# A decoder kernel of twelve layers: the last feed-forward in bf16 terms, the ternary feed-forward by groups, and shared statistics in the last cross attention

## The chip, the cores and the metric

The kernel runs on one core of one Trainium2 chip. The engines of a core work side by side and are ordered by semaphores: PE (TensorE, matrix products and transposes), DVE (VectorE), ACT (ScalarE), POOL (GpSimd) and SP (SyncE, which issues DMAs here). The metric is the device time of one execution in microseconds, as the median of several runs.

## The reference

`x` has 2 x 1024 tokens of 256 features. Twelve layers follow each other, four blocks of attention, cross attention and feed-forward, each as `x = layernorm(x + layer(x))` with eps 1e-5 and no gain. Three of them, and the norms between them, are touched by the change.

The feed-forward of the second block quantises its activations to 8 bits per token and its weights to three values:

```python
def bitlinear(x, w, b):
    xn = rmsnorm(x)                    # x * rsqrt(mean(x*x) + 1e-6)
    xq = activation_quant(xn)          # round(xn * 127/max|xn|), clipped, divided again
    wq = weight_quant(w)               # -1, 0, 1 times mean|w|
    return einsum('bsi,oi->bso', xq, wq) + b
h = gelu(bitlinear(x, w1, b1)); out = bitlinear(h, w2, b2)      # 256 -> 1024 -> 256
```

The cross attention of the last block normalises `x` (which has just been normalised by the block's layernorm) a second time, with a gain and a bias, makes queries from it, and keys and values both from it and from a context of 154 masked rows of 192 features. Queries and keys are normalised per head (4 heads of 64); the output is projected and `bo` is added.

The feed-forward of the last block has weights quantised to -1, 0 and 1 without a scale, and activations in full precision:

```python
def _quantize(W):
    gamma = mean(abs(W))
    return clip(round(W / (gamma + 1e-5)), -1.0, 1.0)
h = relu(einsum('bsd,fd->bsf', x, _quantize(W1)) + b1)          # 256 -> 1024
out = einsum('bsf,df->bsd', h, _quantize(W2)) + b2              # 1024 -> 256
```

## The kernel before

`x` stays in SBUF through all layers as 16 tiles (NT) of 128 tokens by 256 features in float32. A layer's method does the layer; `run` calls them in turn and loads the next layer's weights while one works (`after_loads`, which returns the next layer's weights). After each residual addition `stats` makes a tile's mean and variance (`mv`). Where a layer isn't `by_tile` or `grouped`, `run` then calls `post_norm`: one square root on ACT for all 16 tiles, one reciprocal on DVE, and sixteen DVE operations `(x - mean) * r` in place, 128x256 each. A layer named in `LAZY` is left without it, and the next layer does the norm itself. `centred` is the same operation for one tile with a given `r`, and `twin_roots` makes both roots that two norms in a row need from one set of variances, by integer and Newton steps on DVE alone; both were there for the first feed-forward.

A scheduler orders the instructions of each engine from the program's order, their dependencies and a cost model. `in_order(since)` binds PE to the program's order; this is done in several stages, the last cross attention among them, and not in the two feed-forwards here. PSUM is given out as banks by name: four `pa`, two `pt`, two `po` in the feed-forwards.

`l1_ffn` works on four groups of four tiles. `first(g)` takes the absolute maxima of the group (L1352), scales to 8-bit integers in float32 (`xq`, L1357), rounds (L1359) and casts to bf16 (`xi`, L1348), and POOL adds the output's bias `b2` to `x` (L1358). `second` transposes a tile on PE, multiplies by the bf16 ternary weights, scales and biases `h` on DVE (L1376), and does the GELU and the sums of squares on ACT. `third`, one group later, quantises `h`, transposes and multiplies again and adds to `x` (L1395). `first(g + 1)` is called after all four tiles of group `g`.

`l3_xattn` prepares the context (`l3_context`, `l3_turned_context`), the pairs of tiles (`l3_pair`: statistics, root on POOL by a power, `xn` on DVE at L2202, `bo` added to `x` on POOL at L2204, transposes, ACT with gain and bias at L2211, then keys and values in `l3_keys`) and queries (`l3_queries`). These are generators that `flights` takes a step at a time. The root of the context, `crs`, is also POOL's (L2117, L2119). Then come 8 units of ten blocks of keys: scores on PE, exponentials on ACT (L2329), products with the values (L1898), DVE sums (`acc`, L1903) and the next unit's maxima on PE and DVE (L2290). The rest of the preparation, `later`, is taken in steps between the blocks.

`l3_ffn` transposes `x` to `xT` (`start_features`, 16 tiles), quantises both weights in place in float32 (`ternary`: absolute sum L1293, then three operations L1298 to L1300 over 128x2048), and for each of four groups of 512 tokens does eight products of 128x512 (two float32 matmuls each) with ReLU on ACT (L1946), then four tiles of eight float32 products and one for the bias row (`row_pair`), added to `x` at L321. After it `run` normalises all tiles (L329) and issues sixteen output DMAs on SP (L2844).

## Time and profile before

| what | us |
|---|---|
| runs: median (lowest to highest of 3) | 3605.53 (3596.46 to 3615.26) |
| the profiled execution, its own time | 3597.27 |
| its span | 3595.5 |
| mean granted PE clock | 0.908 |
| busy: PE / DVE / ACT / POOL | 3086.0 / 1739.3 / 1274.3 / 398.1 |
| start of l1_ffn: reciprocal of the norm / first `xi` | 1915.33 / 1932.88 |
| last cross attention: first norm operation / first context root used | 3008.30 / 3023.22 |
| last feed-forward: first / last matmul product | 3455.58 / 3582.98 |
| first output DMA issued | 3585.23 |

Rows of a group read: line, engine, operation, output <- inputs, shapes, count, then busy time and mean ns of one, then idle time of the engine just before them with what ended it. Rows of a timeline read: start, duration, engine, line, operation, names, shapes, count, and in brackets the idle time before with its releaser. PEld is the weight load of PE. A busy PE is not PE at its peak, since ends of matmuls are modelled.

### The profile page before, as it was taken

The page shows a single profiled execution, that of the slowest core. Times are in us where ns is not written, and L with a number is a line of the kernel's source. Part 1 is how long each engine was busy: PE and PEld are TensorE (multiplying, and loading weights), DVE is VectorE, ACT ScalarE, POOL GpSimd, SP SyncE. Part 2 cuts the span into 40 slices and gives each one's busy share as a digit, 9 for nine tenths or more (in the row PEclk, how much of TensorE's full clock was granted, in tenths as well). Part 3 has the DMA queues.
Part 4 walks back from the last instruction along what each step waited for, and adds up shares of the span by engine and source line. Part 5 has one row for each costly group of instructions (what it writes and reads, how often), then busy time and mean ns, then how long its engine had stood idle before and what let it go on. Part 6 is the DMA issues. An engine that isn't in the chain of part 4 may idle for free.

```text
span 3595.5 us, 57974 instructions
## 1 busy us (share of the span) xinstructions
PE 3086.0 (86%) x24289; PEld 1896.1 (53%) x24296; DVE 1739.3 (48%) x3889; ACT 1274.3 (35%) x2319; POOL 398.1 (11%) x510
## 2 busy tenths in 40 slices
PE   8997889989959997688895699999798786899978
PEld 3554556654459997576432456454475343443345
DVE  2366775434541112797668665100201765567741
ACT  3553345434411111597344523111022443333321
POOL 0000000010012332100001131000021202110000
PEclk9998779789969999799997799999799897999989
DMA  3234523100058886000000001100133000000000
GB/s 96 80 83 124 130 73 88 34 1 1 24 205 322 316 326 220 1 2 33 1 1 8 8 1 72 59 0 0 57 129 127 19 1 27 1 1 1 1 0 24
DMA packets 152542, 242.19 MB, mean 67 GB/s; under 512 B 47059, under 2 KB 127450, under 8 KB 147290
## 3 DMA queue, kind: packets, MB, share of 16 engines
q1 hardware_dynamic: 140874, 115.67, 10.9%
q0 software_dynamic: 11408, 122.83, 8.9%
q8 instruction: 191, 3.13, 0.4%
q14 instruction: 69, 0.57, 0.1%
HBM read 195.07 MB, written 43.38 MB: 66 GB/s over the span
## 4 chain that ended last, share of the span: by engine, by line
PE 71%; DVE 17%; ACT 5%; issue 3%; POOL 2%; DMA 2%; SPq 0%; POOLq 0%; DVEq 0%; ACTq 0%
PE pa L253 29%; PE po L253 9%; PE po L1898 2%; PE wide L741 2%; PE wide L2324 2%; PE pa L1573 2%; PE po L823 1%; PE wide L2289 1%; PE wide L253 1%; PE pt L295 1%; PE px L253 1%; PE po L2584 1%; PE y_ps L2637 1%; PE pa L1459 1%; PE wide L711 1%
## 5 line engine op out<-in xcount | busy, mean ns | idle before, releaser
L253 PEld LDWEIGHTS pa<-xgT,ew 128*128 128x128 f32 x2184 | 251.7, 193 | 2.8 <-DVE xgT L967 0.8
L253 PE MATMUL pa<-xgT,ew 128*128 128x128 f32 x2184 | 252.0, 276 | 0.4 <-DVE xgT L967 0.4
L253 PE MATMUL pa<-xT,w 128*128 128x512 f32 (+3 forms) x488 | 236.6, 627 | 4.0 <-DVE x L321 1.8
L253 PE MATMUL pa<-ha,w 128*128 128x512 f32 x512 | 220.4, 592 | 0.0
L985 DVE TENSOR_TENSOR hid<-a,pa 128x512 f32<-128x512 f32 x78 | 48.4, 621 | 294.6 <-ACT a L984 294.6
L253 PEld LDWEIGHTS pa<-ha,w 128*128 128x128 f32 x512 | 97.3, 190 | 122.5 <-issue 122.5
L746 ACT ACTIVATE e<-wide 77x1024 f32<-77x1024 f32 x128 | 124.2, 1016 | 104.4 <-PE wide L741 101.3
L2744 DVE COPY lg<-po 128x8 f32<-128x8 f32 x16 | 2.7, 167 | 302.1 <-PE po L2741 302.1
L253 PE MATMUL po<-w,h 128*128 128x256 f32 (+1 forms) x640 | 144.5, 382 | 0.0
L253 PEld LDWEIGHTS pa<-xT,w 128*128 128x128 f32 (+2 forms) x488 | 87.1, 190 | 105.9 <-issue 97.0
L253 PEld LDWEIGHTS po<-w,h 128*128 128x128 f32 (+1 forms) x640 | 113.2, 179 | 30.6 <-issue 8.5
L984 ACT ACTIVATE a<-pa 128x512 f32<-128x512 f32 x78 | 42.4, 544 | 234.1 <-PE pa L253 234.1
L253 PE MATMUL po<-ew,hid 128*128 128x256 f32 x546 | 125.3, 379 | 0.0
L295 PE MATMUL pt<-cst,x 128*128 128x128 f32 x224 | 52.1, 339 | 82.4 <-DVE x L2079 53.8
L715 DVE TENSOR_REDUCE m<-wide 128x4 f32<-128x616 f32 x128 | 95.6, 792 | 44.8 <-PE wide L711 44.6
L2329 ACT ACTIVATE e<-wide 128x1024 f32<-128x1024 f32 x64 | 65.5, 1023 | 116.9 <-PE wide L2324 116.2
L253 PEld LDWEIGHTS po<-ew,hid 128*128 128x128 f32 x546 | 100.2, 190 | 11.8
L2290 DVE TENSOR_REDUCE m<-wide 128x2 f32<-128x1024 f32 (+1 forms) x96 | 90.7, 968 | 18.3 <-PE wide L2289 18.3
L1147 ACT ACTIVATE e<-cst,wS,nS 128x80 f32<-128x80 f32 x256 | 95.3, 449 | 0.0
L2289 PE MATMUL wide<-kT,qT 64*128 64x512 f32 (+1 forms) x384 | 86.5, 532 | 6.6 <-DVE m L2290 5.7
L1580 ACT ACTIVATE hb<-pa,cols 128x512 f32<-128x512 f32 x32 | 22.0, 687 | 197.8 <-PE pa L253 197.8
L1903 DVE TENSOR_TENSOR acc<-acc,e 128x1024 f32<-128x1024 f32 (+1 forms) x64 | 78.1, 1221 | 27.4 <-ACT e L2329 19.7
(649 smaller groups left out, 6430.4 us busy)
## 6 DMA issues: line engine op xcount, KB each, us to landing
w<-in_L2f_eW_dram SPq DMA_DIRECT2D x16, 1024.0 KB, 6.4
pk<-pk SPq DMA_DIRECT2D x96, 128.0 KB, 2.2
rw<-pk SPq DMA_DIRECT2D x64, 128.0 KB, 2.7
y<-yd SPq DMA_DIRECT2D x16, 512.0 KB, 5.5
ld<-lgs SPq DMA_DIRECT2D x64, 64.0 KB, 2.2
li<-ld SPq DMA_DIRECT2D x16, 256.0 KB, 4.7
md<-mi SPq DMA_DIRECT2D x32, 128.0 KB, 3.8
mt<-md SPq DMA_DIRECT2D x64, 64.0 KB, 1.8
```

What stands on the lines that cost most here:

```text
L253: self.nc.tensor.matmul(out, l, r, start=(i == 0), stop=(i == n - 1))
L295: self.nc.tensor.transpose(ps[:, c * 128:(c + 1) * 128], src[:, c * 128:(c + 1) * 128], self.ident)
L715: nc.vector.tensor_reduce(m[:, t, 2 * k:2 * k + 2, G0:G0 + 2], s, AX.X, ALU.max)
L741: nc.tensor.matmul(pair[j // 2][:KH, j % 2 * 512:j % 2 * 512 + 512], kp[R, G, o:o + KH], tiles[g][R, G], start=True, stop=True)
L746: nc.scalar.activation(s, pair[k][:KH], AF.Exp, scale=0.25)
L1147: nc.scalar.activation(e[:, 4 * j + G], self.k("rel"), AF.Tanh, scale=nS[:, i, h:h + 1], bias=wS[:, i, h:h + 1])
L1573: nc.tensor.matmul(ps, w["rW1"][:, c, m * 128:(m + 1) * 128], self.xT[:, c, cols], start=(c == 0), stop=(c == 1))
L1898: nc.tensor.matmul(av[a * 64:a * 64 + 64], v[:rows, n, h:h + 64], e[:rows, a * 512:a * 512 + 512], start=(s == 0), stop=(s == 9))
L1903: nc.vector.tensor_tensor(acc[:rows], acc[:rows], e[:rows], ALU.add)
L2289: nc.tensor.matmul(wide[:, a * 512:a * 512 + size], qT[R, c, o:o + 128], kT[R, c, keys], start=(n < 2), stop=True)
L2290: nc.vector.tensor_reduce(m[:, t, :, n], wide.rearrange("p (a k) -> p a k", a=2)[:, :, :size], AX.X, ALU.max)
L2324: nc.tensor.matmul(wide[:rows, a * 512:a * 512 + 512], kT[R, c, o:o + rows], qT[R, c, q], start=False, stop=True)
```

## The change

Five things change, in this order of the diff.

`l1_ffn`: the layer before it, `l1_xattn`, becomes lazy; the root is made at the start of `l1_ffn`, and the tiles are centred group by group in `first(g)`. The bias is added by one DVE operation per group, `biased(g)`, called after the group's first tile, in place of four POOL operations; `first(g + 1)` is called after the group's second tile.

`l3_xattn`: `l3_attn` becomes lazy; `twin_roots` makes the roots of the block's norm and of the layer's own norm. `l3_pair` makes `xn` from the raw `x` with the one root, and normalises `x` in place with the other; POOL still adds `bo`.

`l3_weights`: the quantisation of the last feed-forward's weights is handed to the attention's `later`, in steps over halves of 128x1024, and ends in bf16 in the place of the float32 weights.

`l3_ffn`: the features and the hidden values are split into three bf16 terms each (`terms`: a difference, a cast, a difference on DVE, where ACT has written the highest term), and each product is six (up) or 24 (down) bf16 matmuls. The bias `b2` is added to `x` by POOL, 128x256 each. The down products of a group come after the up products of the next group and the transposes of the one after, and PE is bound to this order.

The end: `l3_ffn` is lazy, and each tile gets its root, its norm and its output DMA in the loop, one tile behind.

```diff
@@ -1338,7 +1338,9 @@
             ms = p1.tile([128, NT], F, name="ms")
             top = p1.tile([128, NT], F, name="top")
 
-            nc.vector.tensor_tensor(ms, self.norm, self.norm, ALU.mult)
+            norm = p1.tile([128, NT], F, name="norm")
+            self.rstd(norm, self.mv[:, :, 1], self.eps5)
+            nc.vector.tensor_tensor(ms, norm, norm, ALU.mult)
             nc.vector.tensor_tensor(ms, ms, self.mv[:, :, 1], ALU.mult)
             nc.vector.tensor_scalar(ms, ms, 1e-6, None, ALU.add)
             ms = self.newton_root(p1, ms, NT)
@@ -1349,17 +1351,22 @@
 
             def first(g):
                 tiles = slice(g * 4, g * 4 + 4)
+                for i in range(g * 4, g * 4 + 4):
+                    self.centred(self.x[:, i], i, norm[:, i:i + 1])
                 nc.vector.tensor_reduce(top[:, tiles], self.x[:, tiles], AX.X, ALU.max, apply_absolute_value=True)
                 sc = self.l1_scales(p, ms[:, tiles], top[:, tiles], g1)
                 xq = p.tile([128, 4, D], F, name="xq")
                 for k in range(4):
                     i = g * 4 + k
                     nc.vector.tensor_scalar(xq[:, k], self.x[:, i], ms[:, i:i + 1], sc[:, k:k + 1], ALU.mult, ALU.mult)
-                    nc.gpsimd.tensor_tensor(self.x[:, i], self.x[:, i], w["b2"], ALU.add)
                 nc.vector.tensor_scalar(flat(xq), flat(xq), -128.0, ROUND, ALU.max, ALU.add)
                 xi = p.tile([128, 4, D], BF, name="xi")
                 ints(flat(xi), flat(xq))
                 return xi
+
+            def biased(g):
+                tiles = slice(g * 4, g * 4 + 4)
+                nc.vector.tensor_tensor(self.x[:, tiles], self.x[:, tiles], w["b2"].unsqueeze(1).to_broadcast([128, 4, D]), ALU.add)
 
             def second(g, k, xi, hm, ht):
                 i = g * 4 + k
@@ -1395,7 +1402,7 @@
                 nc.vector.scalar_tensor_tensor(self.x[:, i], ps[:, :D], ht[:, k:k + 1], self.x[:, i], ALU.mult, ALU.add)
                 self.finish(i)
 
-            behind = None
+            behind = ahead = None
             xi = first(0)
             for g in range(5):
                 if g < 4:
@@ -1407,8 +1414,11 @@
                         hs.append(second(g, k, xi, hm, ht))
                     if behind:
                         third(g - 1, k, *behind[k])
-                if g < 3:
-                    xi = first(g + 1)
+                    if k == 0 and g < 4:
+                        biased(g)
+                    if k == 1 and g < 3:
+                        ahead = first(g + 1)
+                xi = ahead
                 if g < 4:
                     nc.vector.tensor_scalar(hm, hm, 1e-6, None, ALU.add)
                     hm = self.newton_root(p, hm, 4)
@@ -1834,7 +1844,7 @@
 
 
         nc, tc = self.nc, self.tc
-        after_loads()
+        following = after_loads()
         self.psum_close()
         cp = self.psum_cx = ExitStack()
         PS = bass.MemoryType.PSUM
@@ -1845,6 +1855,7 @@
         with ExitStack() as cx:
             p1 = cx.enter_context(tc.tile_pool(name="x1", bufs=1))
             p = cx.enter_context(tc.tile_pool(name="x2", bufs=2))
+            self.twin = self.twin_roots(p1, 1e-5)
             k = self.l3_context(p1)
             qT = p1.tile([128, 2, T], F, name="qT")
             batches = [(p.tile([128, 2, SK + S], F, name="kT"), p.tile([128, 10, D], F, name="v")) for _ in range(B)]
@@ -1873,6 +1884,8 @@
             self.bank = self.pa
             later = self.flights([query(4), query(6)] + pairs(1) + [self.l3_keys(p, 1, 0, batches[1], w, k)]
                                      + [query(i) for i in range(8, NT, 2)], 3)
+            weights = self.l3_weights(p1, following)
+            later = (x for g in (later, (x for _ in weights for x in (True, True))) for x in g)
             order = list(range(2, 10)) + [0, 1]
             score = lambda u, s, sh: self.l3_scores(p, units[u], order[s], qT, batches[units[u][0]], k, sh)
             behind, oT = [], None
@@ -1928,26 +1941,74 @@
         w = {m: self.load(s, self.ins[f"L3f_{m}"]) for m in ("W1", "W2")}
         w["raw1"] = s[0][:, 0:2048]
         w["raw2"] = s[0][:, 2048:4096]
-        w["b2"] = self.rows(s, "L3_ffn_b2", D)
+        w["b2"] = self.rows_all(s, "L3_ffn_b2", D)
+        w["spare"] = s[0][:, 4096 + D:4608 + D]
         return w
 
     def l3_ffn(self, w, after_loads):
+
+
         nc, tc = self.nc, self.tc
         after_loads()
-        self.start_features()
+        rs = self.rs
+        since = len(nc.cur_bb.bb.instructions)
         with tc.tile_pool(name="t1", bufs=2) as p:
-            self.ternary(p, w["raw1"], w["raw1"], 1024 * D, True)
-            self.ternary(p, w["raw2"], w["raw2"], 1024 * D, True)
-            for g in range(4):
-                h = p.tile([128, 8, 512], F, name="h")
+            self.rstd(rs, self.mv[:, :, 1], self.eps5)
+
+            def features(g):
+                xt = [p.tile([128, 2, 512], BF, name=f"xt{j}") for j in range(3)]
+                for i in range(g * 4, g * 4 + 4):
+                    nc.vector.tensor_scalar(self.x[:, i], self.x[:, i], self.mv[:, i, 0:1], rs[:, i:i + 1], ALU.subtract, ALU.mult)
+                for k in range(4):
+                    i = g * 4 + k
+                    tile_of = slice(k * 128, k * 128 + 128)
+                    pt = self.transpose_pair(self.x[:, i])
+                    v = self.xT[:, :, i * 128:(i + 1) * 128]
+                    nc.scalar.copy(v, pt)
+                    nc.scalar.copy(xt[0][:, :, tile_of], pt)
+                    self.terms([t[:, :, tile_of] for t in xt], v, high=False)
+                for i in range(g * 4, g * 4 + 4):
+                    nc.gpsimd.tensor_tensor(self.x[:, i], self.x[:, i], w["b2"], ALU.add)
+                return xt
+
+            def up(g, xt):
+                h = [p.tile([128, 8, 512], BF, name=f"h{j}") for j in range(3)]
                 for m in range(8):
                     ps = self.pa()
-                    self.mm(ps, [(w["W1"][:, c, m * 128:(m + 1) * 128], self.xT[:, c, g * 512:(g + 1) * 512]) for c in range(2)])
-                    nc.scalar.activation(h[:, m], ps, AF.Relu, bias=self.col("L3_ffn_b1", m))
+                    self.mm(ps, [(w["q1"][:, c, m * 128:(m + 1) * 128], t[:, c]) for c in range(2) for t in xt])
+                    f = p.tile([128, 512], F, name="f", bufs=3)
+                    nc.scalar.activation(f, ps, AF.Relu, bias=self.col("L3_ffn_b1", m))
+                    nc.scalar.activation(h[0][:, m], ps, AF.Relu, bias=self.col("L3_ffn_b1", m))
+                    self.terms([t[:, m] for t in h], f, high=False)
+                return h
+
+            def ended(i):
+                nc.vector.tensor_scalar(self.x[:, i], self.x[:, i], self.mv[:, i, 0:1], rs[:, i:i + 1], ALU.subtract, ALU.mult)
+                nc.sync.dma_start(self.out[i * 128:(i + 1) * 128], self.x[:, i])
+
+            def down(g, h):
                 for k in range(4):
+                    i = g * 4 + k
                     ps = self.po()
-                    self.mm(ps[:, :D], [(h[:, m, k * 128:(k + 1) * 128], w["W2"][:, m]) for m in range(8)] + [self.row_pair(w["b2"])])
-                    self.residual(g * 4 + k, ps[:, :D])
+                    self.mm(ps[:, :D], [(t[:, m, k * 128:(k + 1) * 128], w["q2"][:, m]) for m in range(8) for t in h])
+                    nc.vector.tensor_tensor(self.x[:, i], self.x[:, i], ps[:, :D], ALU.add)
+                    self.stats(i)
+                    nc.scalar.activation(rs[:, i:i + 1], self.mv[:, i, 1:2], AF.Sqrt, bias=self.eps5)
+                    if i:
+                        ended(i - 1)
+                    nc.vector.reciprocal(rs[:, i:i + 1], rs[:, i:i + 1])
+                ended(i) if i == NT - 1 else None
+
+            xt = features(0)
+            behind = up(0, xt)
+            xt = features(1)
+            for g in range(1, 5):
+                h = up(g, xt) if g < 4 else None
+                if g < 3:
+                    xt = features(g + 1)
+                down(g - 1, behind)
+                behind = h
+            self.in_order(since)
 
     NB = 2 * NT + NE - 1
 
@@ -2192,15 +2253,13 @@
 
         nc = self.nc
         i = b * TPB + 2 * j
-        r = self.rs[:, i:i + 2]
-        for t in range(2):
-            self.stats(i + t)
-        self.inverse_root(r, self.mv[:, i:i + 2, 1], self.eps5.to_broadcast([128, 2]), 2)
-        yield True
+        r = self.twin
         xn = p.tile([128, 2, D], F, name="xn", bufs=3)
         for t in range(2):
-            nc.vector.tensor_scalar(xn[:, t], self.x[:, i + t], self.mv[:, i + t, 0:1], self.rs[:, i + t:i + t + 1],
-                                    ALU.subtract, ALU.mult)
+            self.centred(xn[:, t], i + t, r[:, 1, i + t:i + t + 1])
+        yield True
+        for t in range(2):
+            self.centred(self.x[:, i + t], i + t, r[:, 0, i + t:i + t + 1])
             nc.gpsimd.tensor_tensor(self.x[:, i + t], self.x[:, i + t], w["bo"], ALU.add)
         yield True
         ps = self.bank()
@@ -2814,12 +2873,52 @@
     def centred(self, dst, i, r):
         self.nc.vector.tensor_scalar(dst, self.x[:, i], self.mv[:, i, 0:1], r, ALU.subtract, ALU.mult)
 
+    def l3_weights(self, pool, w):
+
+        nc = self.nc
+        w["q1"] = w["raw1"][:, 0:1024].bitcast(BF).rearrange("p (c n) -> p c n", n=1024)
+        w["q2"] = w["raw2"][:, 0:1024].bitcast(BF).rearrange("p (c n) -> p c n", n=D)
+        keep = w["spare"].bitcast(BF)
+        for n in (1, 2):
+            raw, q = w[f"raw{n}"], w[f"q{n}"]
+            r = pool.tile([128, 4], F, name=f"tern{n}")
+            for k in range(2):
+                nc.vector.tensor_reduce(r[:, k:k + 1], raw[:, k * 1024:k * 1024 + 1024], AX.X, ALU.add, apply_absolute_value=True)
+                yield True
+            nc.vector.tensor_tensor(r[:, 2:3], r[:, 0:1], r[:, 1:2], ALU.add)
+            yield True
+            ps = self.pa()
+            self.mm(ps[:, 0:1], [(self.k("ones"), r[:, 2:3])])
+            nc.vector.tensor_scalar(r[:, 3:4], ps[:, 0:1], 1.0 / (D * 1024), 1e-5, ALU.mult, ALU.add)
+            nc.vector.reciprocal(r[:, 3:4], r[:, 3:4])
+            yield True
+            flat = q.rearrange("p c n -> p (c n)")
+            for k in range(2):
+                half = raw[:, k * 1024:k * 1024 + 1024]
+                nc.vector.tensor_scalar(half, half, r[:, 3:4], 1.0, ALU.mult, ALU.min)
+                yield True
+                nc.vector.tensor_scalar(half, half, -1.0, ROUND, ALU.max, ALU.add)
+                yield True
+                nc.vector.tensor_scalar(flat[:, 1024:2048] if k else keep, half, -ROUND, None, ALU.add)
+                yield True
+            nc.vector.tensor_copy(flat[:, 0:1024], keep)
+            yield True
+
+    def terms(self, dst, src, high=True):
+
+        nc = self.nc
+        if high:
+            nc.vector.tensor_copy(dst[0], src)
+        nc.vector.tensor_tensor(src, src, dst[0], ALU.subtract)
+        nc.vector.tensor_copy(dst[1], src)
+        nc.vector.tensor_tensor(dst[2], src, dst[1], ALU.subtract)
+
 
     LAYERS = ("l0_attn", "l0_xattn", "l0_ffn", "l1_attn", "l1_xattn", "l1_ffn",
               "l2_attn", "l2_xattn", "l2_ffn", "l3_attn", "l3_xattn", "l3_ffn")
 
 
-    LAZY = ("l0_xattn",)
+    LAZY = ("l0_xattn", "l1_xattn", "l3_attn", "l3_xattn", "l3_ffn")
 
     def run(self):
         loads = [getattr(self, "load_" + n) for n in self.LAYERS]
@@ -2840,8 +2939,6 @@
             if not self.fed and name not in self.LAZY:
                 self.post_norm()
             w = nxt[0] if nxt else None
-        for i in range(NT):
-            self.nc.sync.dma_start(self.out[i * 128:(i + 1) * 128], self.x[:, i])
         self.psum_close()
```

## The prediction

> **What bounds the kernel now.** I read the page's head and the chain of waits first, then tables by stage for the four places that the change touches, then groups and timelines there.
>
> ```profile
> PE 3086.0 (86%) x24289; PEld 1896.1 (53%) x24296; DVE 1739.3 (48%) x3889; ACT 1274.3 (35%) x2319; POOL 398.1 (11%) x510
> PE 71%; DVE 17%; ACT 5%; issue 3%; POOL 2%; DMA 2%; SPq 0%; POOLq 0%; DVEq 0%; ACTq 0%
> ```
>
> PE carries the chain as a whole, but these shares say little of single stages. In the table by stage the columns are the stretch, its length, the busy time of PE, PEld, DVE, ACT and POOL, and the granted clock:
>
> ```profile
> 1910.00:1934.00 24.00, 3.51 (x19) 2.81 (x18) 22.07 (x69) 1.05 (x2) 3.93 (x5) 0.64 0.10 28
> 3326.00:3361.00 35.00, 32.41 (x168) 11.10 (x168) 26.58 (x29) 12.42 (x14) 0.00 (x0) 1.00 0.01 1
> 3440.00:3456.00 16.00, 4.96 (x17) 3.47 (x18) 14.99 (x31) 1.42 (x4) 0.00 (x0) 0.50 0.00 1
> 3456.00:3583.00 127.00, 126.99 (x436) 78.45 (x434) 20.22 (x54) 23.62 (x37) 0.00 (x0) 0.99 0.00 0
> 3583.00:3596.00 13.00, 0.00 (x0) 0.00 (x0) 6.54 (x20) 0.31 (x1) 0.00 (x0) 0.60 0.48 161
> ```
>
> Start of l1_ffn (row 1): DVE bound. One unit of the last cross attention (row 2): PE bound, DVE 8 us free. Last feed-forward: 16 us DVE bound at half clock, 127 us pure PE, and a tail of 13 us without PE. The groups of the last stage, and its end:
>
> ```profile
> L253 PE MATMUL po<-w,h 128*128 128x256 f32 x256 | 59.1, 384 | 0.0
> L253 PE MATMUL pa<-xT,w 128*128 128x512 f32 x128 | 58.6, 609 | 0.0
> L1946 ACT ACTIVATE h<-pa,cols 128x512 f32<-128x512 f32 x32 | 22.0, 687 | 83.8 <-PE pa L253 83.8
> L1293 DVE TENSOR_REDUCE tr<-w 128x1 f32<-128x2048 f32 x2 | 4.6, 2276 | 0.0
> ...
> 3583.02 0.42 DVE L321 TENSOR_TENSOR x<-x,po 128x256 f32<-128x256 f32 x1 [3.18 <-PE po L253]
> 3584.79 5.25 DVE L329 TENSOR_SCALAR x<-x,mv,rs 128x256 f32<-128x256 f32 x16
> 3585.23 7.74 SPq L2844 DMA_DIRECT2D out_dram<-x  x16
> ```
>
> Rows that price the new operations: bf16 matmuls at half clock (8 in 3.60 us) and at full clock (8 in 1.05 us), and DVE beside a working POOL and alone.
>
> ```profile
> 1942.75 3.60 PE L253 MATMUL pa<-w,xqT 128*128 128x512 bf16 x8 [4.82 <-ACT xqT L1370]
> 1965.99 1.05 PE L253 MATMUL po<-w,hT 128*128 128x256 bf16 x8 [0.99 <-ACT hT L1392]
> 1928.56 2.19 DVE L1357 TENSOR_SCALAR xq<-x,root,qsc 128x256 f32<-128x256 f32 x4
> 1929.05 2.96 POOL L1358 TENSOR_TENSOR x<-x,w 128x256 f32<-128x256 f32 x4 [130.58 <-DVE xq L1357]
> 1932.88 0.68 DVE L1348 TENSOR_SCALAR xi<-xq 128x1024 bf16<-128x1024 f32 x1
> L1903 DVE TENSOR_TENSOR acc<-acc,e 128x1024 f32<-128x1024 f32 x6 | 7.3, 1222 | 1.9 <-ACT e L2329 1.9
> ```
>
> A DVE scaling of 128x256 costs 0.33 us in a run (5.25/16) and 0.55 beside POOL (2.19/4).
>
> **A. l1_ffn.** Before, recip at 1915.33, 16 scalings (5.25), four reductions of 1.21 and the Newton steps put the first xq at 1928.56; POOL's four bias adds (0.72 each) then stretch xq by 0.22 x 4 and the next small operations to 0.68, so xi comes at 1932.88. After, twelve scalings and three reductions fit ahead of xq (−0.33 x 4 −1.2 = −2.5; some small operations fall into gaps, −0.9), and without POOL xq, 1359 and xi shrink by about 2; the new bias addition of 128x1024 (1.22) stands between. First xi −4. The remaining group's work comes later, where PE waits for DVE, and takes 1 back. Groups 2 and 3 lose the contention of POOL (two rows of 3.44 us) for one addition of 1.22: −1.5 each. Sum −6; bounds −9 (nothing is taken back) and −3 (only the lead-in's scalings count).
>
> **B. Last cross attention's lead-in.** Before: last aggregate 3007.6, then sqrt, recip, 16 scalings to 3013.5, statistics anew, POOL power 0.72 per pair; POOL's crs ends 3023.18 and holds the context (DVE idle 3.85 us). After: 13 small dependent DVE operations at 0.21 (2.7), then 20 scalings, half in place, for ten tiles; each in-place one frees a POOL add of bo (0.72). Ten of these stand in POOL's queue before the mask casts (2.4) and crs (1.2): from 3011 to 3018–3021, crs at 3022–3024.7, against 3023.2. So DVE's earlier end is not passed on; late next is crs. Four ternary reductions (1.21) lie here in the idle of DVE. Behind it POOL has no eps and power per pair (0.19+0.72) ahead of the query roots, worth 0 to 4. Two table loads and one sqrt less are off the path. I take −2; bounds −6, +3.
>
> **C. Ternary weights moved into the attention loop.** Removed from the last stage: two reductions 2.28, six scalings of 128x2048 (1.2–1.27) on DVE, of which 4.6+3.7 stood before the first transposes. Added: in each of two units a burst of six scalings 128x1024 (0.60) and a bf16 copy, 4.2 us. A unit is 34.7 us with DVE 26.6–27.1 busy; its chain alternates PE, DVE maximum, ACT, so a burst delays some maximum: +2 each, +4. Bounds 0 (it fits into 8 us idle) and +9 (fully exposed). The scale's matmul with the ones waits for DVE's sum, and the scores of the next unit are queued behind it on PE; the sum is 0.2 us and a step earlier, so I cost it at nothing, and at 1.2 (one DVE addition in front) without that cover.
>
> **D. Last feed-forward, up and down.** Lead-in: before, last residual ends 3439.2, first up matmul 3455.6 (16.4). After: statistics 0.61, sqrt 0.31, recip 0.25, six scalings 2.0, then per tile transposes, two ACT copies 0.37, DVE difference, cast, difference of 128x256 (0.9) with two scalings between: 8 us to the first up. Gain 8.4; bounds 4 (tile pitch 1.15 at half clock, as the copies at 3450.28 and 3451.43 had) and 9.5.
>
> PE: a group's up is 48 bf16 matmuls of 128x512; half of the half-clock 0.43 is 0.215, 10.3 us (before 13.8). A down tile is 24 of 0.12 (1.05/8 = 0.13 with one start in it), 2.9, four 11.5, against 4.27 x 4 = 17.1. DVE per m: difference 0.61 (half of 1.22), cast 0.34 (half of 0.68), difference 0.61 = 1.56, more than PE's 1.29 or ACT's two relus at 0.69. First group to second up: nothing else covers, so DVE sets it: 2.7 + 8 x 1.56 + four tiles at 0.9 = 18.8. Middle steps: up 10.3, transposes waiting for ACT 3.9, down 11.5 = 25.7, twice; DVE has 12.5+4+6.4 = 23 there and stays just below. Last: 10.3+11.5+11.5 = 33.4. Sum 103.6. PE waits some 6 us after the first up; such a wait (idle to 3449.5) left it at half clock until 3458, so +2. POOL now adds b2 (16 x 0.72), and beside it DVE runs 1.7 times as long: +2. Total 107.6 against 127.4 (3455.6 to 3583.0): −19.8; bounds −27 (no wait, full clock) and −8 (per m 1.9, steps 28).
>
> [...]
>
> **E. Tail.** Before 12.5 us from last PE end 3583.0 to 3595.5: residual to aggregate 1.1, sqrt and recip 0.6, then sixteen DMA issues 7.74 and 2.5. After, fourteen tiles are gone by then; the last: 1.1 + 0.6, two scalings 0.7 (the tile before goes first), one issue 0.5, 2.5 = 5.4. Gain 7.1; bounds 5 (an earlier transfer is still queued) and 8. Inside the stage each tile's recip now waits for ACT's sqrt (0.31), with DVE's next differences queued behind it; the scaling of the tile before covers it, and without that cover it is 16 x 0.35, inside R1's margin. SP has nothing else queued.
>
> **Sum.** −6 −2 +4 −8.4 −19.8 −7.1 = −39.3, on the profiled execution's 3597.27: 3558.0. That execution lies 8.3 below the median 3605.53, near the lowest of the three shown (3596.46 to 3615.26); against the median the sum gives 3566. I take 3562, midway, and put the rivals on the same base, 3601. A measurement of this kernel tells about 0.5% (18 us) from no change.
>
> **Rivals.** R1, DVE becomes the bound of the last stage: with 2.3 us per m (1.5 times, near the contended ratio) DVE needs 32 x 2.3, 16 x 1 for features, 16 x 1.6 for residual, statistics and scaling, and 2.7: 118; D's middle gains 9, the bursts cost 9: −6 −2 +9 −8.4 −9 −7.1 = −24, 3577. For: DVE's margin is only 2.7 us a step. Against: POOL works 2.9 us a group only.
> R2, three times the matmuls eat what bf16 saves: bf16's 0.215 x 6 = 1.29 per m against 1.72 leaves little, and if DVE's and ACT's waits leave steps near 31 only lead-in, tail and A's lower bound count, with C at +9: −9.5, within 0.5%, 3592. Against: the 1.05 us row.
> R3, slower: the last stage runs like l1_ffn, whose bf16 matmuls with waits between had 8 in 3.60 us. At 0.45 and 0.236 a step is 21.6+22.7+4 = 48; four give 193, +66, less lead-in, tail and A to C: +46, 3647. It decides once the stage's mean granted clock is below 0.61: 97 us of PE work / 0.61 + 6.6 = 165, which is 127.4 + 15.5 + 4 + 18. Against: PE has 24 us of work in 26.
>
> **How the numbers follow.** Likeliest 0.60, its own range 3545 to 3579 (the bounds of A to E added in squares, about 13, and half the distance of the two bases, 4). R1 0.20, R2 0.11, R3 0.09. Range 3538 to 3594: it takes R1 and most of R2, leaves R3 and a tenth below out. Faster by over 0.5% is below 3587.5: the first, most of R1, little of R2: 0.80; within 0.5% 0.12; slower 0.08.
>
> **What would show it.** Right: first up about 8 us after the last residual; second up 19 later; steps of 25 to 27 with PE busy over 90% and a clock near 1; last PE to end 5 us; first h of l1_ffn 4 to 6 earlier; units with a burst 36 to 37 long. Wrong: DVE busy without a break over the last stage, a clock below 0.7 there, or units 5 us longer, or crs later than the sum of the lead-in.

## The result, and the profile after

The changed kernel takes 3568.64 us (median of 5 runs, 3564.39 to 3574.31) against 3605.53 us (5 runs, 3596.46 to 3615.26). The ratio is 0.991 with a 95% interval of 0.988 to 0.994. The prediction was 3562 us in a range of 3538 to 3594.

The profiled execution has a span of 3565.6 us (before 3595.5) and a mean granted clock of 0.904 (before 0.908). The first row of its page:

```profile
PE 3062.2 (86%) x24445; PEld 1882.0 (53%) x24456; DVE 1802.5 (51%) x4036; ACT 1301.2 (36%) x2387; POOL 413.1 (12%) x494
```

PE has 24 us less to do and DVE 63 us more. Where the time went is read from the starts and ends of the instructions that bound each stage, in the timelines of both profiled executions. "Unit" is one of the eight units of the last cross attention, and a unit ends where ACT's copy of its products (`avs`) begins.

| stretch | before | after | difference | predicted |
|---|---|---|---|---|
| start to the last statistic of l1_xattn (no change in it) | 1914.95 | 1920.81 | +5.86 | |
| A: from there to the first query copy of the next layer | 153.17 | 149.28 | -3.89 | -6 (-9 to -3) |
| from there to the last residual of l3_attn (no change in it) | 938.63 | 938.03 | -0.60 | |
| B: from there to the end of unit 0 | 135.80 | 130.29 | -5.51 | -2 (-6 to +3) |
| unit 1 | 61.45 | 61.45 | 0 | 0 |
| C: units 2 to 7 | 219.77 | 232.41 | +12.64 | +4 (0 to +9) |
| from there to the last residual of l3_xattn | 15.45 | 15.45 | 0 | 0 |
| D: from there to the last PE instruction | 143.77 | 112.78 | -30.99 | -28.2 |
| E: from there to the end | 12.51 | 5.06 | -7.45 | -7.1 |

The five changed stretches sum to -35.2 us; the prediction had -39.3. Over all the profiled executions of this study the first stretch lies between 1893 and 1926 us, with the same code in it. The changed stretches repeat within 0.1 us where their code is the same, but for two: B, which has two levels (130.2 to 130.9 and 132.5 to 132.8 us), and D, which lies between 112.0 and 113.1. In five of the seven kernels with the higher level of B the unchanged stretch ahead of it is about 2 us shorter (935.4 to 935.8 against 937.7 to 938.1), so there B and that stretch together come out the same. So the experiments below are read by stretch and not by a whole time.

The tables by stage of the changed kernel, for the places that the prediction showed (columns as there; the stretches are l1_ffn's start, units 3 and 5, and the lead-in, body and tail of the last feed-forward):

```profile
1916.00:1938.00 22.00, 4.47 (x21) 3.14 (x21) 19.08 (x68) 3.04 (x5) 0.00 (x0) 0.65 0.12 31
3250.48:3290.38 39.90, 34.77 (x168) 11.80 (x168) 30.42 (x38) 12.18 (x14) 0.00 (x0) 0.92 0.00 0
3333.14:3369.52 36.38, 33.80 (x166) 11.45 (x166) 26.57 (x29) 12.17 (x14) 0.00 (x0) 0.95 0.01 1
3447.72:3457.85 10.13, 4.12 (x11) 1.76 (x13) 9.65 (x27) 2.71 (x9) 3.05 (x4) 0.50 0.00 1
3457.85:3560.50 102.65, 90.90 (x593) 59.51 (x595) 87.33 (x213) 51.22 (x103) 31.78 (x12) 0.95 0.06 19
3560.50:3565.60 5.10, 0.01 (x1) 0.00 (x0) 1.61 (x5) 0.29 (x1) 0.00 (x0) 0.87 0.15 51
```

Row 3 is a unit in which nothing of the change runs (DVE as busy as before, 26.57), and still it is 1.64 us longer than before, at a clock of 0.95 instead of 1.00. Row 5 is the last feed-forward's body: PE busy for 89%, DVE for 85%, the clock 0.95. The groups of that stage, and from the timeline of DVE its end:

```profile
L253 PE MATMUL pa<-xt,w 128*128 128x512 bf16 x188 | 47.1, 407 | 8.7 <-DVE xt L2913 6.3 <-POOL x L1971 0.8 <-ACT xt L1968 0.7
L253 PE MATMUL po<-w,h 128*128 128x256 bf16 x384 | 42.4, 273 | 0.0
L295 PE MATMUL pt<-cst,x 128*128 128x128 f32 x32 | 6.8, 325 | 9.5 <-ACT xt L1968 7.0 <-DVE x L1961 2.3
L1971 POOL TENSOR_TENSOR x<-x,w 128x256 f32<-128x256 f32 x16 | 34.8, 2204 | 282.4 <-PE pt L295 282.4
L2912 DVE TENSOR_TENSOR f<-f,h 128x512 f32<-128x512 f32 x32 | 21.9, 684 | 6.6 <-ACT h L1981 6.6
L2913 DVE CAST h<-f 128x512 bf16<-128x512 f32 x32 | 13.4, 420 | 0.3
```

```profile
3560.61 0.42 DVE L1994 TENSOR_TENSOR x<-x,po 128x256 f32<-128x256 f32 x1 [0.55 <-PE po L253]
3562.28 0.41 DVE L1986 TENSOR_SCALAR x<-x,mv,rs 128x256 f32<-128x256 f32 x1
```

The products take 47.1 + 42.4 = 89.5 us where they took 58.6 + 59.1 = 117.7, and PE sits idle in two places: 8.7 us before up products, and 9.5 us before the transposes, of which 7.0 are waits for ACT's copies. The down products wait for nothing. After the last of them there are 5 us instead of 12.5, because fourteen tiles are out by then.

The part that went wrong is C. Its rows before and after, and PE at the end of unit 2 of the changed kernel:

```profile
3204.00:3423.77 219.77, 204.53 (x994) 73.21 (x994) 162.61 (x199) 75.56 (x85) 4.85 (x3) 0.98 0.00 1
3199.86:3432.27 232.41, 212.76 (x998) 75.72 (x998) 170.44 (x217) 75.64 (x84) 4.86 (x3) 0.95 0.00 1
3245.45 0.40 PE L2365 MATMUL pa<-identb,pad 128*128 128x128 bf16 x4 [1.64 <-DVE pad L2360]
```

And this is DVE in unit 3, with the scores of the next unit on PE:

```profile
3278.29 1.42 DVE L2898 TENSOR_SCALAR w<-w,tern 128x1024 f32<-128x1024 f32 x2
3279.62 1.28 DVE L2900 TENSOR_SCALAR w<-w 128x1024 f32<-128x1024 f32 x2
...
3282.35 0.16 DVE L2358 TENSOR_REDUCE mr<-m 128x8 f32<-128x24 f32 x1
...
3282.44 0.67 DVE L2902 TENSOR_SCALAR w<-w 128x1024 bf16<-128x1024 f32 x1
...
3283.14 0.69 DVE L2902 TENSOR_SCALAR w<-w 128x1024 bf16<-128x1024 f32 x1
...
3283.84 0.42 DVE L2904 COPY w<-w 128x1024 bf16<-128x1024 bf16 x1
...
3284.83 0.61 PE L2365 MATMUL pa<-identb,pad 128*128 128x128 bf16 x4 [2.60 <-DVE pad L2360]
3286.49 1.94 PE L2383 MATMUL wide<-qT,kT 64*128 64x512 f32 x4
...
3293.68 1.23 DVE L1914 TENSOR_TENSOR acc<-e 128x1024 f32<-128x1024 f32 x1 [7.80 <-ACT e L2388]
```

The scalings of the weights stand on DVE just ahead of the "shift" of the next unit (the maxima that its scores need, a chain of six small operations from L2358 to the last L2360, 0.16 to 0.19 us each), and in unit 3 the last two and the copy stand between the operations of the chain. PE waits 2.60 us for its end (1.64 in unit 2), and the four score products after it take 1.94 instead of 1.02 us. The granted clock is half in these stretches of the loop (the clock is the last column but two), each 3.4 us long or three times that:

```profile
3246.80:3250.20 3.40, 3.40 (x10) 0.51 (x6) 0.00 (x0) 1.02 (x1) 0.00 (x0) 0.51 0.00 0
3284.40:3294.60 10.20, 9.10 (x26) 3.04 (x28) 2.36 (x4) 3.22 (x4) 0.00 (x0) 0.50 0.00 0
3304.90:3308.30 3.40, 3.19 (x8) 0.93 (x8) 3.33 (x6) 0.00 (x0) 0.00 (x0) 0.50 0.00 0
3349.20:3352.60 3.40, 3.40 (x10) 1.10 (x12) 2.19 (x2) 0.00 (x0) 0.00 (x0) 0.51 0.00 0
3383.40:3386.80 3.40, 3.40 (x12) 1.34 (x10) 2.42 (x5) 0.00 (x0) 0.00 (x0) 0.50 0.00 0
```

That makes seven windows of 3.4 us. The kernel before had two in the same loop, at 3299.0 (unit 4) and 3374.1 (unit 6).

The records of the clock show when such a window came. In the profiled executions of both kernels every change of the clock (107 in each) lies on a grid with a step of 3.413 us, within 0.02 us. In their units 2 to 7, the seven steps at full clock in which PE by the profile sat idle for 1.86 to 2.32 us in all are followed by half clock, and the others, with at most 1.48 us, are not; in run 5 one step with 1.86 us was not either. So in this loop it matters where the grid cuts a wait. PE waits about 1.87 us for DVE in unit 5 of both kernels, here in the changed one:

```profile
3348.05 1.13 PE L2348 MATMUL wide<-kT,qT 64*128 64x512 f32 x4 [1.87 <-DVE m L2349]
```

Here the whole wait lies in one step (from 3345.82) and the next step is at half clock. In the kernel before, a border of the grid at 3339.95 cuts the same wait into 0.59 and 1.28 us, and the clock stays full.

### The profile page after: what moved, and what is told of

It reads as the page before. It is cut to its first block, busy times and chain, and to the rows that moved or that the text cites. A ratio compares the mean times of both kernels' runs of the same rounds, so it can differ in the third digit from the quotient of the medians.

```text
span 3565.6 us, 58543 instructions
## 1 busy us (share of the span) xinstructions
PE 3062.2 (86%) x24445; PEld 1882.0 (53%) x24456; DVE 1802.5 (51%) x4036; ACT 1301.2 (36%) x2387; POOL 413.1 (12%) x494
## 5 line engine op out<-in xcount | busy, mean ns | idle before, releaser
L253 PE MATMUL pa<-xT,w 128*128 128x512 f32 (+3 forms) x360 | 173.5, 620 | 3.9 <-DVE x L321 1.8
L253 PE MATMUL po<-w,h 128*128 128x256 bf16 (+2 forms) x768 | 127.7, 326 | 0.0
L253 PEld LDWEIGHTS pa<-xT,w 128*128 128x128 f32 (+2 forms) x360 | 61.4, 184 | 77.2 <-issue 69.8
L1911 PE MATMUL po<-e,v 128*64 128x512 f32 (+1 forms) x320 | 89.9, 641 | 0.2 <-ACT e L2386 0.2
```

The lines of the kernel that those rows point to most:

```text
L253: self.nc.tensor.matmul(out, l, r, start=(i == 0), stop=(i == n - 1))
L1911: nc.tensor.matmul(av[a * 64:a * 64 + 64], v[:rows, n, h:h + 64], e[:rows, a * 512:a * 512 + 512], start=(s == 0), stop=(s == 9))
```

## The experiments

**Theories.** For C the theory is that the place of the work costs the time: a burst in front of the shift makes PE wait, and the wait halves the clock for a while after. The rival is that the loop has no room for 4.2 us more on DVE in a unit, wherever it stands. For A: the loss of 2.1 us against the prediction lies in a table load that the new place of the square root exposes. For D: PE's waits are made by POOL's bias additions beside DVE, or by the order of features and up products. For B: the gain comes from the shared statistics. All kernels start from the changed kernel; all but the last two change one thing in it.

**1. The quantisation back in the last feed-forward** (C undone alone).

```diff
-            weights = self.l3_weights(p1, following)
-            later = (x for g in (later, (x for _ in weights for x in (True, True))) for x in g)
...
+            for _ in self.l3_weights(p, w):
+                pass
             self.rstd(rs, self.mv[:, :, 1], self.eps5)
```

> The changed kernel with the quantisation of the last feed-forward's weights taken out of the attention loop and done at the start of that feed-forward. Measured are the six last units of the loop (from the second to the eighth copy of the values' sum on ACT): 219.77 us before the change, 232.41 after. Theory 1 (the bursts of six scalings stand on DVE ahead of the next unit's shift, PE waits some 3 us twice, and its clock halves behind each wait): the loop is back at 219.5 to 221. Theory 2 (the loop grew for another reason of the change, such as the shared statistics or the order of the rest of the preparation): it stays above 228. Both: the lead-in of the feed-forward, last residual to the unbroken run of up matmuls 10.1 us after, grows by the reductions (4 x 1.2) and the bursts (2 x 4.2) less what hides, to 17 to 23; so the sum with the bursts out of the loop is 0 to 5 us faster or slower than the changed kernel.

Units 2 to 7 took 221.39 us, and from the last residual to the end 128.79 instead of 117.85:

```profile
3187.17:3408.56 221.39, 206.16 (x994) 74.11 (x994) 162.64 (x199) 75.54 (x85) 4.85 (x3) 0.98 0.00 1
```

So the bursts cost 11.0 us in the loop and save 10.9 us behind it. As it is placed, the move of the quantisation is worth nothing. The remaining 1.6 us over the kernel before are all in unit 5 (36.38 us at a clock of 0.95, as in the changed kernel). This kernel has no moved work in the loop, and its unit 5 has the changed kernel's length, clock and busy time of PE (33.80 us), so these 1.6 us go with the half-clock window there and are no cost of the bursts.

**2. Whole bursts right behind the shift.** The steps are called late in each unit; in the trace the two bursts stand at the start of units 3 and 6.

```diff
-            later = (x for g in (later, (x for _ in weights for x in (True, True))) for x in g)
...
                     for _ in range(2):
                         next(later, None)
+                    if u > 1 and s in (8, 9):
+                        for _ in range(2):
+                            next(weights, None)
```

> The changed kernel with each burst of the quantisation moved a few blocks, so that it stands on DVE right behind a unit's shift, where DVE sat idle for 6 us before the first sum of a unit. The work and its engine are the same. Theory 1 (place and clock): the six last units of the loop fall from 232.4 to 219.8 to 222, and the half-clock windows in the loop go from five back to two. Theory 2 (DVE's 8.8 us of added work are paid wherever they stand): 228 to 233.

The loop took 225.19 us, 7.2 less than 232.41, with as much work on DVE:

```profile
3205.20:3430.39 225.19, 207.29 (x998) 74.27 (x998) 171.21 (x217) 75.55 (x84) 4.86 (x3) 0.98 0.00 1
```

The result lies between the two theories' numbers. Units 2, 4 and 5 are as before (46.71, 40.81 and 34.74). The two units with a burst keep 3.5 us (unit 3) and 2.0 us (unit 6): the little product that gives the scale stood behind two score blocks on PE, and DVE lost 2.31 us waiting for it before it could begin. The half-clock windows are three instead of seven. So most of the cost is the place, and a burst of this size still does not fit whole.

**3. Four half bursts behind four shifts,** each with a scale product of its own, and the sums taken early (shortened).

```diff
                     if s == 8 and m is not None:
                         ahead = self.l3_shift(p, u + 1, m, k)
+                        if u > 1:
+                            next(weights, None)
...
+        def halves():
+            for n in (1, 2):
+                raw, r = w[f"raw{n}"], rs[n - 1]
...
+                for k in range(2):
+                    half, s = raw[:, k * 1024:k * 1024 + 1024], r[:, 3 + k:4 + k]
+                    ps = self.pa()
+                    self.mm(ps[:, 0:1], [(self.k("ones"), r[:, 2:3])])
...
+                    yield True
```

> The changed kernel with the quantisation in four half bursts (three scalings of 128x1024, some with the bf16 copy, 2 us), each with its own small matmul for the scale and each on DVE right behind the shift of one of the units 2 to 5. The run with whole bursts behind the shift gave 225.2 us for the six last units: there the scale's matmul stood behind two score blocks on PE, and 2.3 us of DVE's idle passed before the burst began. Theory 1 (place, and clock behind the waits): a burst of 2 us fits into the 6 us of idle and the loop is 219.8 to 221. Theory 2 (every microsecond of added DVE work costs PE at least its half): 224 or more.

The loop took 222.59 us, 9.8 less; units 2 to 6 are 47.03, 35.05, 41.10, 36.65 and 40.87. The table row of the loop, and the place of one half burst:

```profile
3183.42:3406.00 222.58, 207.34 (x1002) 74.50 (x1002) 173.30 (x221) 75.48 (x84) 4.85 (x3) 0.98 0.00 1
```

```profile
3262.88 0.38 PE L253 MATMUL pa<-tern,cst 128*128 128x1 f32 x2 [0.68 <-ACT sh L2369]
...
3263.69 0.75 DVE L2905 TENSOR_SCALAR w<-w,tern 128x1024 f32<-128x1024 f32 x1
...
3265.21 0.69 DVE L2907 TENSOR_SCALAR w<-w 128x1024 bf16<-128x1024 f32 x1
3267.74 1.23 DVE L1914 TENSOR_TENSOR acc<-e 128x1024 f32<-128x1024 f32 x1 [1.84 <-ACT e L2390]
```

DVE does 2.9 us more here than in the changed kernel, and the loop is shorter. Three of the four units with a half burst grow by 0.2 to 0.3 us over the kernel before, and DVE still waits 1.84 us after the burst for the first exponentials. Unit 5 has 1.9, of which 1.64 is the window of run 1. The loop again ended between the two theories' numbers (at most 221, or 224 and more), 1.6 us above the first, which is that window. So the theory of the place holds but for it: the room is there, behind the shift, while PE and ACT start the next unit.

**4. The same work on POOL.**

```diff
-                nc.vector.tensor_scalar(half, half, r[:, 3:4], 1.0, ALU.mult, ALU.min)
+                nc.gpsimd.tensor_scalar(half, half, r[:, 3:4], 1.0, ALU.mult, ALU.min)
... (the other two scalings and the copy in the same way)
```

> The changed kernel with the twelve scalings and two copies of the quantisation on POOL, which has nothing to do in the last five units. Theory 1: DVE's order is that of before, so the loop is 220 to 222 if POOL takes nothing from DVE; by the rows of l1_ffn before the change (scalings 0.33 us alone, 0.55 beside POOL) DVE's operations beside POOL's some 30 us stretch by up to 1.7 and the loop is 224 to 236. Theory 2 (the amount of DVE work): 220 to 222.

The table row of the loop, and groups of units 2 and 3:

```profile
3204.21:3436.99 232.78, 213.38 (x998) 75.65 (x998) 166.77 (x203) 75.63 (x85) 48.38 (x17) 0.95 0.00 1
```

```profile
L2900 POOL TENSOR_SCALAR w<-w 128x1024 f32<-128x1024 f32 x4 | 14.5, 3632 | 0.0
L2360 DVE CAST pad<-mr 128x8 bf16<-128x8 f32 x3 | 1.3, 434 | 0.1
L2362 DVE TENSOR_TENSOR mr<-mr,pad 128x8 f32<-128x8 f32 x2 | 1.2, 608 | 0.1
```

No gain: 232.78. DVE is relieved, but a scaling takes POOL 3.6 us, and beside it the shift's small operations at the end of unit 3 take 0.43 and 0.61 us on average, where each took 0.16 to 0.19; one of each kind takes about 1. The shift is late again, and the clock is again 0.95. What is late on PE decides, and not which engine does the scaling.

**5. PE kept busy during the wait.** If the clock is the second half of the cost, useless bf16 transposes of the identity in front of the shift's transposes must take that half back and leave the wait.

```diff
         ps = self.psa.tile([128, 8, 128], BF, name="pa")
+        for t in range({3: 14, 4: 22}.get(u, 0)):
+            nc.tensor.transpose(ps[:, 4 + t % 4], k["ident"], k["ident"])
```

> The changed kernel with useless transposes of a constant (14 and 22 of 128x128 in bf16, into an unused part of the bank) on PE where it waits for the shift that the bursts delay, at the end of the units 2 and 3. DVE's work, its order and the length of the waits stay; PE is busy in them. Theory 1a (of the 12.6 us that the loop grew, more than half is the half clock behind the two waits): the loop of the six last units falls from 232.4 to 223 to 227, and its mean granted clock from 0.95 up to 0.98. Theory 1b (the delay of the shift itself is the price, and the clock only goes with it): 230 to 233.

The table row of the loop, and PE's timeline at the end of unit 3:

```profile
3172.33:3398.90 226.57, 209.15 (x1034) 76.22 (x1034) 170.35 (x217) 75.62 (x84) 4.85 (x3) 0.98 0.00 1
```

```profile
3252.98 1.40 PE L2365 MATMUL pa<-identb 128*128 128x128 bf16 x22
3255.64 0.40 PE L2367 MATMUL pa<-identb,pad 128*128 128x128 bf16 x4 [1.26 <-DVE pad L2360]
```

The loop fell by 5.8 to 226.57 us although PE got 36 instructions more. The windows are three, units 4 and 5 are as before (40.81 and 34.73), and units 2 and 3 keep 2.2 and 4.6 us. So of the 12.64 us, 5.8 went with PE's idleness, as lost clock (46%, where the theory named more than half), and 6.8 are delay that stays, some of it still at half clock (one window more than before). Of the 5.8 us, 1.65 are those of unit 5 (34.73 against 36.38), which is without its window here. The 22 transposes filled only 1.40 us, and 1.26 of the wait was left open in unit 3. How the 4.6 us of that unit divide into the wait and what follows from it was not taken further apart.

**6. The root of l1_ffn in its old memory.** The tile `norm` lies in a pool whose memory POOL had used, so the square root waits for two semaphores, DVE's and POOL's (before, for DVE's alone). In the changed kernel ACT's timeline has

```profile
1920.89 1.28 ACT L366 ACT_TABLE_LOAD   x1 [5.59 <-DVE mv L363]
1922.18 0.31 ACT L366 ACTIVATE norm<-mv,cst 128x16 f32<-128x16 f32 x1
```

that is, the table load stands behind the wait for the last statistic (1920.81). Before, it was done (1909.46 to 1910.74) while ACT waited for that statistic (until 1914.96).

```diff
-            norm = p1.tile([128, NT], F, name="norm")
+            norm = self.sp.tile([128, NT], F, name="rs")
```

> The changed kernel with the root of l1_ffn's norm in the long-lived pool that the norm after a layer used, instead of in the layer's own pool, where its memory was POOL's before. Theory 1: the second wait (for POOL) had put the wait for DVE's statistics on the load of ACT's table, so the load of 1.28 us began only after them; it goes back behind other work, last statistics to root 1.4 us earlier, and the stage ends 1.0 to 1.5 us earlier. Rival: what comes earlier is taken back where PE and ACT set the pace of the groups, and the stage ends within 0.3 us of where it did.

The same two instructions on ACT's timeline:

```profile
1918.99 1.28 ACT L366 ACT_TABLE_LOAD   x1
...
1924.52 0.31 ACT L366 ACTIVATE rs<-mv,cst 128x16 f32<-128x16 f32 x1 [4.25 <-DVE mv L363]
```

The load is done 4.25 us before it is needed, the first `xi` comes 13.10 us after the last statistic (14.43), and stretch A is 146.31 us (149.28). That is 2.97 us, twice what was expected. The 1.33 us at the start explain less than half. PE's busy time in the stage falls from 80.3 to 78.2 us at a clock of 0.74 (0.73), so part of the rest is clock too; it was not tested by itself.

**7. The layer's own statistics back** (B undone alone).

```diff
-            self.twin = self.twin_roots(p1, 1e-5)
...
-    LAZY = ("l0_xattn", "l1_xattn", "l3_attn", "l3_xattn", "l3_ffn")
+    LAZY = ("l0_xattn", "l1_xattn", "l3_xattn", "l3_ffn")
...
+        for t in range(2):
+            self.stats(i + t)
+        self.inverse_root(r, self.mv[:, i:i + 2, 1], self.eps5.to_broadcast([128, 2]), 2)
```

> The changed kernel with the last cross attention's start as before: the block's norm for all tiles behind the attention, statistics and POOL's power per pair of tiles, one scaling per tile. The stretch from the last residual of the attention to the first copy of the values' sum was 135.8 us before and 130.3 to 132.6 in the runs since. Theory 1 (the shared statistics take the power per pair out of POOL's queue): 134 to 137.5, 3 to 6 us longer, with the context scaled 1 to 3 us earlier than with the change (16 to 18 us after the residual against 18.5 to 18.9). Theory 2 (the gain is only a different phase of PE's half-clock windows): 130 to 133.

Stretch B is 135.95 us (before 135.80, changed 130.3 or 132.7), and the context is scaled 16.47 us after the last residual, as before, instead of 18.90. So the shared statistics bring 3.2 to 5.7 us, and they bring it although the context comes 2.4 us later. With the unchanged stretch ahead of it included it is 1075.2 us here and 1074.4 before the change, against 1067.9 to 1068.7 in ten of the twelve kernels with shared statistics and 1071.3 and 1071.8 in the other two.

**8. Features of the second group ahead of the first up products.**

```diff
             xt = features(0)
+            xt1 = features(1)
             behind = up(0, xt)
-            xt = features(1)
+            xt = xt1
```

> The changed kernel with the second group's transposes and splits called ahead of the first group's up products, so that the second up products need not wait for the eight splits of the first. Theory (the prediction's: DVE sets the way from the first group to the second, 18.8 us by the sum): first up matmul to second group's first falls from 24.5 to 12 to 16, and last residual to PE's end from 112.8 to 104 to 109; part comes back as waits for hidden values (psum and the three buffers of f) in the second group. Rival (PE's half clock and the steps' own pace set it): PE's end stays within 2 us.

The last PE instruction came 112.11 us after the last residual, 0.7 earlier, which is the rival's number (within 2 us) and not the theory's (104 to 109). On PE:

```profile
3459.67 21.52 PE L253 MATMUL pa<-xt,w 128*128 128x512 bf16 x93 [0.22 <-DVE xt L2914]
...
3488.45 0.66 PE L295 MATMUL pt<-cst,x 128*128 128x128 f32 x2 [7.05 <-DVE x L1961]
```

The wait between the first and the second group's up products is gone (93 products in one run), but PE waits 3.85 us ahead of them and 7.05 us behind them, where the next scalings stand on DVE behind sixteen splits of the hidden values. By these waits DVE's work up to the first down products sets this end, and reordering PE moves the wait only.

**9. No addition of `b2`,** and **10. the additions later,** behind the last ReLU of the group's up products.

```diff
-                for i in range(g * 4, g * 4 + 4):
-                    nc.gpsimd.tensor_tensor(self.x[:, i], self.x[:, i], w["b2"], ALU.add)
                 return xt
...
(in run 10 alone, at the end of up; `last` is ACT's last instruction up to there:)
+                for i in range(g * 4, g * 4 + 4):
+                    nc.gpsimd.tensor_tensor(self.x[:, i], self.x[:, i], w["b2"], ALU.add)
+                    self.tc.add_manual_dep(nc.cur_bb.bb.instructions[-1], last.name, how, reason="bias behind the products")
```

> The changed kernel without the sixteen additions of b2 on POOL in the last feed-forward (the bias is left out of the output). Theory of the prediction: POOL's additions stretch DVE's work beside them, 2 us in all: PE's end 1.5 to 2.5 us earlier, all of it in the lead-in, where the first six scalings took 2.85 us beside POOL instead of 2.0. Rival: later additions of POOL, which last 10 us a group in the trace, hold DVE up as well: PE's end 4 us or more earlier.

> The changed kernel with POOL's additions of b2 held back until ACT has done the last ReLU of the same group's up products. Without the additions PE's end came 3.3 us earlier after the last residual (109.5 against 112.8), of which 1.8 lay ahead of the second up matmul. Theory (POOL costs DVE time only where DVE sets the pace, in the lead-in and on the way to the second group): PE's end 110.5 to 111.5, with the second up matmul at 6.9 as without the additions. Rival (an addition of POOL costs the same wherever it stands): 112.3 to 113.

Without the additions PE ended at 109.51 us (3.3 less), with the later ones at 110.24 (2.5 less). In both the second up product came at 6.90 us instead of 8.67. The six scalings of the lead-in, in the changed kernel with POOL beside them and without the additions:

```profile
3449.07 2.85 DVE L1961 TENSOR_SCALAR x<-x,mv,rs 128x256 f32<-128x256 f32 x6
3450.31 3.07 POOL L1971 TENSOR_TENSOR x<-x,w 128x256 f32<-128x256 f32 x4 [241.43 <-PE pt L295]
```

```profile
3425.26 2.02 DVE L1961 TENSOR_SCALAR x<-x,mv,rs 128x256 f32<-128x256 f32 x6
```

The first difference of a feature tile takes 0.95 us beside POOL's additions (3451.84) and 0.42 without them (3427.20). So the contention costs 3.3 us, more than the 1.5 to 2.5 expected, of which 2.5 are had by waiting.

**11 and 12. The mends together:** run 3 with run 6, and these with run 10, six executions each.

> The changed kernel with the half bursts behind the shift and the long-lived root of l1_ffn's norm together. By the single runs the loop gives 9.8 and l1_ffn 3.0 back: 12.8 us, so 3556 against the 3568.6 of the changed kernel, 0.986 to 0.988 of the kernel before. If the two gains overlapped or were phases of the clock only, 3562 or more.

> The same with POOL's additions of b2 held back as well: by the theory of that run another 1.3 to 2.3 us, which the medians of five runs of a kernel that spreads over 10 us can't tell; last residual to the end of the span 115.5 to 116.7 instead of 117.5.

| kernel | median (lowest to highest) | ratio to before, 95% | A | C | D + E |
|---|---|---|---|---|---|
| changed | 3568.64 (3564.39 to 3574.31) | 0.991, 0.988 to 0.994 | 149.28 | 232.41 | 117.85 |
| 3 + 6 | 3546.32 (3534.44 to 3563.07) | 0.985, 0.982 to 0.988 | 146.32 | 222.57 | 117.49 |
| 3 + 6 + 10 | 3539.05 (3528.81 to 3570.88) | 0.985, 0.981 to 0.989 | 146.32 | 222.61 | 116.19 |

The ratios of the last two are to a median of 3598.53 us of the kernel before on the same chip. By the stretches the third kernel is 3.0 + 9.8 + 1.7 = 14.5 us shorter than the changed one; the medians differ by more, but were not taken side by side, and the unchanged first stretch alone varies by 33 us. The third is not told apart from the second by its times; it has 1.3 us less in its last stage. Both ratios' intervals end below the changed kernel's 0.991, whose own interval begins at 0.988, so the stretches and not the ratios carry the comparison.

## Why the prediction was right or wrong

The whole was right (a difference of the medians of -36.9 against a predicted -43.5 on the same base), and "faster by over 0.5%" is what came. That the five stretches came within 4.1 us of the sum (-35.2 against -39.3) is in part luck: C is 8.6 us above its number and A 2.1, and B, D and E are 3.5, 2.8 and 0.3 below theirs. The steps:

- **A, -6: 2.1 us too much, inside its bounds.** The first `xi` comes 3.5 us earlier, against 4. What failed is the silence on the square root: the step counted what DVE does after the reciprocal and not where the root's table load would stand. Run 6 shows that it stands behind the last statistic and is worth 3.0 us.
- **B, -2: too small, near its bound of -6.** "Late next is crs" was right: the context's scaling came 2.4 us later, when the step allowed up to 1.5. That this holds the lead-in was wrong. The work behind it, which the step put at 0 to 4 for POOL's missing powers, gave all of the gain and paid the delay as well: -5.5 in these two executions and -3.1 at the other level of B, in spite of 2.4 us of delay. Run 7 shows that the gain is the shared statistics'; that it is POOL's powers alone was not tested.
- **C, +4: mis-sized, +12.6, outside its bounds of 0 to +9.** The step had a burst delay some maximum by 2 us, took 8 us of free DVE time in a unit as the cover of its lower bound, and made "fully exposed" the upper bound, 4.2 us for each burst. It failed in two ways. It did not ask in front of what the burst stands: the shift, which PE waits for (runs 1 to 4). And its upper bound had only DVE's time in it, while half clock went with the wait for what came after, into the next unit (0.50 from 3284.40 to 3294.60); run 5 puts the clock's part at 5.8 us, of which 1.65 (unit 5) came in run 1 without the bursts too. The prediction's own sign of being wrong, units 5 us longer, came in unit 3 (39.89 against 34.74). The product for the scale, costed at nothing, was right in the changed kernel; in run 2, where the burst stood behind the shift, it cost DVE 2.31 us.
- **D, lead-in, -8.4.** The first up product came at 5.32 us, since a first term alone suffices for it, the second at 8.67 (predicted 8), and products without a break began at 10.13 us. By the first product the gain is 11.0 us, outside the bound of 9.5; by the second it is 7.7. The two terms that were added elsewhere, +2 for the clock and +2 for POOL, are paid largely here: the clock is 0.50 up to 10.13, and of the 3.3 us that run 9 gives for POOL 1.8 lie ahead of the second up product.
- **D, middle, -19.8.** From the first up product to PE's end it took 107.5 us against 107.6, and this agreement is in part luck: the way to the second group took 24.5 us and not 18.8, the last part 31.5 and not 33.4, and the 4 us that had been added for clock and POOL make up the difference. The second group's first up product came at 25.8 us from the last residual and its second at 29.8 (26.8 predicted); from the latter, the next two groups began 27.0 and 24.6 later (25.7), and from there it took 31.5 us to PE's end (33.4). The down products are the term that was too high: 96 took 10.64 us, 0.111 each, and not 0.12, which is 3.5 us over four groups. The pitch of DVE in the first group, 1.54 us an up block, came out as predicted (1.56), since its three operations, 1.78 us together, overlap by 0.08 each.
- **E, -7.1.** -7.45, by the steps as told less one scaling: the tile before the last was scaled by 3560.06, ahead of PE's end at 3560.50. The cover of the square roots inside the stage failed: DVE sat idle for 5.1 us in all before the tiles' reciprocals, waiting for ACT, against the 16 x 0.35 that the step named for that case, and the down products did not wait for it.
- **R1, DVE as the bound,** fell: DVE's differences beside POOL stayed at 0.68 us and its busy share is 85%. They stayed so although POOL works 10.5 us on the additions of a group and not the 2.9 that the prediction named against R1. Where DVE does set the pace (up to the first down products, run 8), it costs PE some 6 us of waits (6.3 in the group's row) and not the stage. **R2, nothing saved,** fell: PE's products went from 117.7 to 89.5 us. **R3, half clock in the last stage,** fell: 0.95 against the 0.61 at which it would decide. Its mechanism was there in the lead-in (0.50), and in the loop of C, where the prediction did not look for it.

The clock was weighed in the prediction for the last stage only. In the loop the half-clock stretches of 3.4 and 10.2 us began behind waits of 1.64 and 2.60 us, with 0.67 for the shift's copy, and 1.86 us of idle time in a step of 3.413 (from 3301.45) were enough. The 5.8 us of run 5 are 0.16% of the span, and yet they are nearly half of the 12.64 us by which C grew.

## What to carry to other kernels

Free time of an engine in a loop is no cover until it is known what stands behind the moved work in that engine's queue: put such work behind the operation that the bound engine waits for next, in pieces that end before the engine is needed again, with their inputs ready early. When PE is the bound, the upper bound of an exposed wait is its length plus the work at half clock that follows it (here 6.8 and 5.8 us of the 12.64). When a first use of a function on ACT moves, look at where its table load lands (1.28 us here) and how many semaphores the activation waits for (two here).

## What the runs showed of the hardware

- Waits of PE of 1.6 and 2.6 us (and 0.67 for the shift's copy behind each) between long runs of products went with half-clock windows of 3.4 us, one and three of them (3246.8, 3284.4). The windows begin on the clock's grid of 3.413 us and not at the end of the wait: 1.35 us after the first (3245.45) and 0.4 us before the end of the second (3284.83). With PE kept busy in the waits one of these four was left. Two of the other three (3304.9 and 3383.4) stand in units 4 and 6, where the kernel before has its two, each at a wait of 2.11 us; the window in unit 5 came where the wait of 1.87 us there lies in one step of the grid (the changed kernel), and not where the grid cuts it into 0.59 and 1.28 us (the kernel before).
- Contention of POOL and DVE goes either way. In the lead-in of the last feed-forward POOL's additions take 0.77 us each and DVE's scalings rise from 0.34 to 0.47. In the body of the stage, beside back-to-back subtractions and casts, DVE keeps its 0.68 and 0.42 us (0.68 to 0.69 and 0.42 to 0.43 from 3460.25 to 3469.80, ahead of the additions) and the same additions on POOL take 2.65 us each (12 in 31.78 us). In the first case DVE pays, in the second POOL.
- A table load of ACT was found in front of the wait of its activation when this waits for DVE alone (run 6), and behind the wait for DVE when it waits for POOL too (the changed kernel, 1.28 us exposed). These are two kernels with one such pair each.
